# Second normalisation from turned rows, and loads dealt out in time, in a two-layer transformer kernel

## The chip, the cores and the metric

The kernel runs on one core of one Trainium2 chip, in one launch. The metric is the device time of the whole program in microseconds (us). The profile is of one execution; its engines are TensorE (PE, with its weight loads as PEld), VectorE (DVE), ScalarE (ACT), GpSimd (POOL) and the queue of SyncE (SPq), which here issues almost all DMAs.

## The reference, cut to what matters

Everything is float32. There are 4096 tokens of 128 features (16 sequences of 256).

```python
x  = L0_attn_x
xn = layernorm(x)                                   # no weights
x  = x + attn0(xn) + ffn0(xn)                       # layer 0
xn = layernorm(x)
x  = x + attn1(xn) + ffn1(xn)                       # layer 1

# attn0: normalises once more, with weights: h = (xn-mean)*rsqrt(var+eps)*ln_g + ln_b
#        8 heads of 64, rotary with scales, windows of 128 with both neighbours, softmax, w_out
# ffn0:  a shared MLP (128 -> 256 -> 128, gelu), and 8 experts of the same size, 2 of them for each token
# attn1: normalises once more, with ln_w and ln_b; u, v, base = silu(h @ uv_w.T + uv_b);
#        u * (relu(q.k/sqrt(128) + bias)^2 @ v) @ o_w.T
# ffn1:  32 experts of 64 with sigmoid gates in 4 groups, 8 for each token, and a shared MLP
```

What the change touches is the normalisation inside `attn0` and `attn1`: its input is already normalised, so its mean is zero and what is left is one factor for each token, `r2 = (var*rs*rs + eps)^-0.5`, where `rs` is the first normalisation's factor.

## The kernel before, in words

The tokens are handled in 8 groups of 512 (`g`). A group is a tile of 128 partitions by 4 chunks (`c`) of 128 features: token `c*128 + p` lies on partition `p`. Matmuls need it turned (features on partitions, 512 tokens along the row), which TensorE does with four 128x128 transposes (`transposed`, L179) into a PSUM bank; ScalarE copies it out.

**Layer 0, attention** (from the start to about 343 us). A loop over `s` from -3 to 64 handles one sequence and one pair of heads in each step; eight steps are a group. The order of the instructions on PE, DVE, ACT and POOL is the order in which they are written (`manual_schedule`); the order of SyncE's DMAs is left to a scheduler at build time. `routed(g)` makes the normalised rows `xn_all`, the factors `r2_all` and the turned rows `xnTs[g]`. `prepare(g)` then makes the input of the projections: `scaled` (L173) multiplies each of the four chunks by its tokens' factors on DVE, PE turns the result (L179), and ACT applies `ln_g` and `ln_b` while it copies the bank into `xhTs` (L358). So each group is turned twice, once as `xn` and once as `xh`. `rotated` makes queries and keys: PE multiplies (`pq`, L381), ACT copies to `here` (L391), four SyncE DMAs exchange halves of 32 partitions into `there` (L394), DVE combines (L398, L402). `load_rest` loads weights and the other groups' inputs, and from step 2 on 20 DMAs of a zero tile (L610) clear `x_rows`.

**Layer 0, experts** (about 346 to 443 us). GpSimd has scattered the tokens into `x_rows`, in 39 tiles of 256 rows, each of one expert. A loop over `t` has four stages, at the distances `at = [0, 4, 5, 6]`: `fetched` (SyncE reads the tile's expert number from a register and loads its weights `we` and its rows `xt`), `turned` (PE, L671; DVE copies to `xT`, L673), `hidden` (PE, L680; ACT gelu), and `down` (PE, L691; DVE adds a bias into `yt`, L698; SyncE stores `yt` to `y_rows`, L699). `we` and `xt` have 6 buffers each, `yt` 4. `rw2` (1 MB) and `rb2` (0.5 MB), which `down` needs, are loaded at `t == 2`. Eleven small weights of layer 1 (`wanted`) are loaded at every third `t`, and after the loop's text come `eg`, `eu` and `ed`, 1 MB each. Here every engine's order, SyncE's too, is the scheduler's.

**Layer 1** (about 443 us to the end). A prologue, in a written order, starts group 0; then a loop over the groups runs 17 pairs of expert matmuls (`g`, `u`, `z`: L960, L962, L997) with pieces of attention (`gau`) and of the next group's preparation (`finish0(g + 1)`) between them. `finish0` gathers the experts' rows, sums them into `x`, normalises (`xn`, L158), computes `r2` (`again`, L169), turns `xn` (L179) into `xnT`, computes `v` and the gates' scores (L791), then `scaled`, four more transposes and ACT's `ln_w1`, `ln_b1` make `xhT` (L817). `route1` chooses experts and spreads their weights over the partitions: a store to memory (L189) and loads that read a row of it for all partitions (`bc`, L865; four buffers, so that the last of a group's eight waits until pair 7 is done). In this loop only POOL's order is written by hand; PE, DVE, ACT and SyncE have the order that the scheduler chose.

Of the kernel before, what the change touches and what calls it, by code (L numbers as in the profile page):

```python
# [11 lines left out]
F32 = mybir.dt.float32  # L12
# [3 lines left out]
ALU = mybir.AluOpType  # L16
# [3 lines left out]
P = 128  # L20
B, N, D = 16, 256, 128
T = B * N
G = 512
# [24 lines left out]
def two_layers(ctx: ExitStack, tc: tile.TileContext, a: dict, out: bass.AP):  # L48
# [114 lines left out]
    def again(r2, var, rs, name):  # L163

        ve = small.tile([P, NC], F32, tag="bve2", name=f"bve2_{name}")
        nc.vector.tensor_tensor(ve, rs, rs, ALU.mult)
        nc.vector.tensor_tensor(ve, ve, var, ALU.mult)
        nc.vector.tensor_scalar(ve, ve, EPS, None, ALU.add)
        nc.gpsimd.tensor_tensor(r2, ve, mhalf, ALU.pow)  # L169

    def scaled(dst, src, r2):
        for c in range(NC):
            nc.vector.tensor_scalar(dst[:, c, :], src[:, c, :], r2[:, c : c + 1], None, ALU.mult)  # L173
# [158 lines left out]
    with first as pa:  # L332
# [17 lines left out]
        xhTs0, vs, oTs, heads, yps = {}, {}, {}, {}, {}  # L350

        def prepare(g):
            xh = wk.tile([P, NC, D], F32, tag="xh", name=f"xh_{g}")
            scaled(xh, xn_all[:, g * NC : (g + 1) * NC, :], r2_all[:, g, :])
            yield
            t = transposed(xh, f"xhT_{g}")
            xhT = wk.tile([P, G], F32, tag="xhT", name=f"xhTs_{g}")
            nc.scalar.activation(xhT, t, AF.Identity, bias=col("ln_b"), scale=col("ln_g"))  # L358
            xhTs0[g] = xhT
            vs[g] = wk.tile([P, NC, 512], F32, tag="v", name=f"v_{g}")  # L360
            yield
# [136 lines left out]
        NS = NG * 8  # L498
        sc, pTs, sms = {}, {}, {}
        order = mybir.EngineType  # L500
        with tc.manual_schedule(engines={order.PE, order.DVE, order.Activation, order.Pool}):
            routing = {g: routed(g) for g in range(NG)}
            preparing = {g: prepare(g) for g in range(NG)}

# [13 lines left out]
            for g in range(NG):  # L518
# [9 lines left out]
                    at = (b, b + 1, b + 2, b + 4, b + 6, b + 8, b + 9, *ranks)  # L528
                for n in at:
                    pieces.setdefault(n, []).append(g)  # L530
            turned_rows = {2: 7, 3: 12, 4: 22, 5: 27, 6: 37, 7: 47}

            step(routing, 0, 3)
            step(preparing, 0, 2)
# [12 lines left out]
            for s in range(-3, NS + 1):  # L547
# [14 lines left out]
                    sm = sms.pop(s + 1)  # L562
                    divided(s + 1, sc[s + 1][0], sm)

                if s == -2:
                    step(preparing, 1)
# [4 lines left out]
                for n in turned_rows:  # L571
                    if turned_rows[n] == s:
                        step(preparing, n)
                if s == 35:
                    placing = places0(wk)
# [62 lines left out]
    with ExitStack() as pb:  # L638
# [15 lines left out]

        def fetched(t):
            read(offs, t, tile_off, (E0 - 1) * P, mybir.EngineType.SP)
            we = wk.tile([P, W0], F32, tag="we", name=f"we_{t}", bufs=6)
            nc.sync.dma_start(out=we, in_=a["ex0"][bass.ds(offs[t], P), :])
            xt = wk.tile([P, 2, D], F32, tag="xt", name=f"xt_{t}", bufs=6)
            ins = nc.sync.dma_start(out=xt, in_=xr[t])  # L660
# [25 lines left out]
        def down(t, we, h):  # L686
            read(offs2, t, tile_w2, (E0 - 1) * 2 * D, mybir.EngineType.PE)
            yp = mm_tile(f"yr_{t}")[:, : 2 * D].rearrange("p (c d) -> p c d", d=D)
            for ch in range(2):
                for c in range(2):  # L690
                    nc.tensor.matmul(  # L691
                        yp[:, ch, :], h[:, c, ch * P : (ch + 1) * P], rw2[:, bass.ds(offs2[t] + c * D, D)],
                        start=(c == 0), stop=(c == 1),
                    )
            y = wk.tile([P, 2, D], F32, tag="yt", name=f"yt_{t}", bufs=4)
            read(offs3, t, tile_off, (E0 - 1) * P, mybir.EngineType.DVE)
            bias = rb2[:, bass.ds(offs3[t], D)].unsqueeze(1).to_broadcast([P, 2, D])
            nc.vector.tensor_tensor(y, yp, bias, ALU.add)  # L698
            nc.sync.dma_start(out=yr[t], in_=y)  # L699

        for g in range(2):
            for _ in shared0(g, wk):
                pass
        stage = [fetched, turned, hidden, down]
        at = [0, 4, 5, 6]
        state = {}

        wanted, w1 = [
# [9 lines left out]
            ("su", [P, P], None),  # L718
            ("sd", [P, D], None),
        ], {}  # L720
        for t in range(NT0 + at[-1]):
            if t == 2:
                rw2 = load("rw2", [P, E0, 2 * D], pool=wk, eng=nc.sync).rearrange("p e d -> p (e d)")
                rb2 = load("rb2", [P, E0 * D], src=a["rb2"].partition_broadcast(P), pool=wk, eng=nc.sync)
            if t % 3 == 0 and t // 3 < len(wanted):
                name, shape, src = wanted[t // 3]
                w1[name] = load(name, shape, src=src, pool=late, eng=nc.sync)
            for f, d in zip(stage, at):
                i = t - d
                if 0 <= i < NT0:  # L730
                    state[i] = f(i, *state.get(i, ()))
        uvu, uvv, uvb, vb, cosr, sinr, biasT, ow, sg, su, sd = (w1[name] for name, _, _ in wanted)
        eg = load("eg", [P, E1 // 2, P], pool=late, eng=nc.sync)
        eu = load("eu", [P, E1 // 2, P], pool=late, eng=nc.sync)
        ed = load("ed", [P, E1 // 2, D], pool=late, eng=nc.sync)


    with ExitStack() as pc:
# [14 lines left out]
        def finish0(g):  # L753
# [24 lines left out]
            again(r2, *normalise(xn, xs[g], *moments(xs[g], f"c{g}")), f"d{g}")  # L778
            nc.gpsimd.tensor_tensor(xs[g], xs[g], xn, ALU.add)
            yield  # L780
            t = transposed(xn, f"xn1T_{g}")
            xnT = wk.tile([P, G], F32, tag="xn1T", name=f"xn1Ts_{g}")
            nc.scalar.copy(xnT, t)
# [3 lines left out]
            if g:  # L787
                v = v1s[g] = wk.tile([P, NC, 256], F32, tag="v1", name=f"v1_{g}")
                for c in range(NC):
                    pv = mm_tile(f"pv1_{g}_{c}")  # L790
                    nc.tensor.matmul(  # L791
                        pv[:, : 256 + E1], xnT[:, c * P : (c + 1) * P], wvr, start=True, stop=True
                    )
                    nc.scalar.copy(sc[:, c, :], pv[:, 256 : 256 + E1])
                    nc.vector.scalar_tensor_tensor(
                        v[:, c, :], pv[:, :256], r2[:, c : c + 1], vbs, ALU.mult, ALU.add
                    )
                    if c % 2:
                        nc.scalar.activation(v[:, c - 1 : c + 1, :], v[:, c - 1 : c + 1, :], AF.Silu)
                    if c == 1:  # L800
                        yield
                sf = sc.rearrange("p c e -> p (c e)")
                nc.scalar.activation(sf, sf, AF.Sigmoid)
            else:
# [312 lines left out]
```

## Time and profile before

| | us |
|---|---|
| median of 6 runs | 940.52 (936.89 to 941.92) |
| the profiled execution | 941.32 |
| its span in the profile | 939.6 |
| PE busy | 893.0 (95%) |
| DVE busy | 695.5 (74%) |
| ACT busy | 495.8 (53%) |
| mean granted TensorE clock | 0.989 of full speed |

Between the span and the execution's own time lie 1.7 us, outside of all engines' work. A row of the timeline gives start, duration, engine, line, operation, output and inputs, and in brackets how long the engine was idle just before and what ended that. A row of the chain gives start, length, and the engine and line on the chain of work that ended last.

### The profile page before, as it was taken

The numbers are of one execution on the slowest core, as the hardware profiler recorded it, in microseconds if no ns is written. First come the engines' busy times: TensorE is split into PE (matmuls) and PEld (weight loads), VectorE is DVE, ScalarE is ACT, GpSimd is POOL, SyncE is SP. The second block draws the span as 40 slices with busy tenths as digits, with TensorE's granted clock in tenths as the row PEclk, the third lists the DMA queues.
The fourth block names the chain that finished last, engine by engine and source line by source line (L and its number), as shares of the span: only waits on it lengthen the run. The fifth ranks groups of instructions, "written<-read, shape, count | busy, mean of one in ns | idle before, by whom it ended". The sixth has DMA issues, their size and how long they took to land.

```text
span 939.6 us, 13471 instructions
## 1 busy us (share of the span) xinstructions
PE 893.0 (95%) x3762; PEld 508.4 (54%) x3762; DVE 695.5 (74%) x2283; ACT 495.8 (53%) x1228; POOL 280.3 (30%) x251
## 2 busy tenths in 40 slices
PE   2899999999999998988999999999999999999997
PEld 1556666555555547987445454454544545445453
DVE  4999999899999933332588587785877858778563
ACT  1788989798799863433443423444234441343411
POOL 2343433322467630000534222242222422221200
PEclk8899999999999999999999999999999999999999
DMA  6171010110122236875063433324333243331430
GB/s 198 26 236 40 23 35 23 24 35 23 44 79 70 64 97 209 249 220 170 29 136 85 104 93 78 91 68 103 96 77 91 65 104 96 75 91 45 104 90 11
DMA packets 69145, 84.54 MB, mean 90 GB/s; under 512 B 14800, under 2 KB 45264, under 8 KB 68560
## 3 DMA queue, kind: packets, MB, share of 16 engines
q1 hardware_dynamic: 64544, 74.76, 30.2%
q0 software_dynamic: 4096, 8.40, 2.8%
q8 instruction: 31, 0.51, 0.2%
q10 hardware_dynamic: 432, 0.53, 0.2%
q14 instruction: 42, 0.34, 0.1%
HBM read 58.22 MB, written 17.04 MB: 80 GB/s over the span
## 4 chain that ended last, share of the span: by engine, by line
PE 64%; DVE 18%; ACT 6%; DMA 4%; issue 3%; SPq 2%; POOL 1%; DVEq 0%; ACTq 0%
PE z L997 9%; PE u L962 8%; PE g L960 8%; PE s L421 5%; PE o L477 4%; DVE p L427 3%; PE yr L691 3%; PE h L680 3%; PE t L460 3%; PE o L935 3%; ACT r1s L901 2%; DVE p L446 2%; PE y L490 2%; PE pq L381 2%; PE pv L365 2%
## 5 line engine op out<-in xcount | busy, mean ns | idle before, releaser
L964 ACT ACTIVATE h<-g 128x512 f32<-128x512 f32 x128 | 75.1, 593 | 204.6 <-PE g L960 201.8
L966 DVE TENSOR_TENSOR h<-h,u 128x512 f32<-128x512 f32 x128 | 86.5, 681 | 61.8 <-PE u L962 46.3
L962 PE MATMUL u<-xn1Ts,eu 128*128 128x512 f32 x256 | 130.8, 592 | 1.2 <-DVE h L966 1.2
L960 PE MATMUL g<-xn1Ts,eg 128*128 128x512 f32 x256 | 130.8, 592 | 0.0
L437 ACT ACTIVATE p<-p,nm 128x256 f32<-128x256 f32 x256 | 127.5, 514 | 0.2 <-DVE nm L427 0.2
L997 PE MATMUL z<-h,ed 128*128 128x512 f32 x224 | 115.3, 598 | 1.7 <-DVE h L969 0.9
L758 POOL DMA_INDIRECT yg<-y_rows,slot_at x64 | 65.7, 1027 | 123.8 <-PE hs L627 105.2
L969 DVE TENSOR_TENSOR h<-h,bc 128x512 f32<-128x512 f32 x128 | 97.7, 770 | 2.3
L427 DVE CUSTOM_DVE_ANT_0 p<-s,mask 128x256 f32<-128x256 f32 x256 | 92.8, 417 | 2.6 <-PE s L421 2.6
L421 PE MATMUL s<-k,q 64*128 64x256 f32 x512 | 84.6, 412 | 9.2 <-DVE k L406 6.3
L962 PEld LDWEIGHTS u<-xn1Ts,eu 128*128 128x128 f32 x256 | 48.5, 190 | 61.2 <-issue 52.4
L460 PEld LDWEIGHTS t<-ident,p 128*128 128x128 f32 x512 | 59.4, 140 | 35.0 <-issue 8.6
L317 POOL DMA_INDIRECT x_rows<-xn_all,slot_at x64 | 67.1, 1048 | 37.0 <-ACT pT L467 16.0
L467 ACT COPY pT<-t 128x512 f32<-128x512 f32 x128 | 69.2, 597 | 10.4 <-PE t L460 10.4
L997 PEld LDWEIGHTS z<-h,ed 128*128 128x128 f32 x224 | 41.4, 190 | 56.0 <-issue 39.2
L960 PEld LDWEIGHTS g<-xn1Ts,eg 128*128 128x128 f32 x256 | 46.9, 190 | 45.3 <-issue 39.5
L906 POOL TENSOR_TENSOR r1s<-r1s,sinr 128x512 f32<-128x512 f32 x16 | 21.0, 1312 | 166.8 <-ACT r1s L901 143.3
L477 PE MATMUL o<-pT,v 128*64 128x256 f32 x512 | 70.1, 395 | 0.3 <-ACT oT L482 0.2
L460 PE MATMUL t<-ident,p 128*128 128x128 f32 x512 | 67.3, 274 | 1.4 <-ACT p L451 1.4
L421 PEld LDWEIGHTS s<-k,q 64*128 64x128 f32 x512 | 51.3, 189 | 27.2 <-DVE nm L427 9.2
L683 ACT ACTIVATE h0s<-h,we 128x256 f32<-128x256 f32 x78 | 32.7, 471 | 59.6 <-issue 36.7
L446 DVE TENSOR_SCALAR p<-p,sm 128x256 f32<-128x256 f32 x208 | 62.1, 357 | 2.3
(264 smaller groups left out, 1516.9 us busy)
## 6 DMA issues: line engine op xcount, KB each, us to landing
bc<-rows_r SPq DMA_DIRECT2D x128, 256.0 KB, 4.2
there<-here SPq DMA_DIRECT2D x128, 64.0 KB, 2.0
we<-in_ex_dram SPq DMA_DIRECT2D x39, 129.0 KB, 2.9
xt<-x_rows SPq DMA_DIRECT2D x39, 128.0 KB, 3.0
y_rows<-yt SPq DMA_DIRECT2D x39, 128.0 KB, 2.6
x_rows<-zero SPq DMA_DIRECT2D x19, 256.0 KB, 3.3
x<-in_x_dram SPq DMA_DIRECT2D x8, 256.0 KB, 5.8
out_dram<-out SPq DMA_DIRECT2D x8, 256.0 KB, 2.3
```

Source lines behind the costliest of these rows:

```text
L421: nc.tensor.matmul(sp[h][:, i, :], q[rows, b, i * P : (i + 1) * P], k[rows, b, :], start=True, stop=True)
L427: nc.vector.tensor_tensor_reduce(out=pr[:, h, i, :], in0=sp[h][:, i, :], in1=mask[:, i, :], scale=-1.0, scalar=-NEG, op0=ALU.add, op1=ALU. ...
L437: paces[1] = nc.scalar.activation(row, row, AF.Exp, bias=nm[:, n : n + 1], scale=-1.0, accum_out=sm[:, n : n + 1])
L446: nc.vector.tensor_scalar(row, row, sm[:, n : n + 1], None, ALU.mult)
L460: nc.tensor.transpose(tp[:, at : at + P], pr[:, h, i, j * P : (j + 1) * P], ident)
L477: nc.tensor.matmul(op[h * DH : (h + 1) * DH, :], vs[g][:, 2 * b + j, (2 * hp + h) * DH : (2 * hp + h + 1) * DH], pT[:, h, j, :], start=(j ...
L960: nc.tensor.matmul(gp, wg, xn1Ts[g], start=True, stop=True)
L962: nc.tensor.matmul(up, wu, xn1Ts[g], start=True, stop=True)
L964: nc.scalar.activation(h, gp, AF.Silu)
L966: nc.vector.tensor_tensor(h, h, up, ALU.mult)
L969: nc.vector.tensor_tensor(h, h, spread_w[g][n // 2][:, n % 2, :], ALU.mult)
L997: nc.tensor.matmul(zp, w, r, start=(n == 1), stop=False)
```

## The change

Four edits go together.

1. For all groups but the first, the second normalisation is applied to the turned rows that are there already. `row_stored` writes the 128x4 factors to memory (16 bytes from each partition), `row_spread` reads that row of 512 back into every partition, and `factored` multiplies the turned rows by it in one DVE instruction, whose second operand it reads with a step of 4 elements. The four `scaled` instructions and the four transposes of each of these groups are gone, in both layers; ACT's affine step now reads SBUF and writes in place.
2. In attention SyncE's order is written too: its DMAs go out in the order of the text.
3. In the expert loop `we` and `xt` have 10 buffers and `yt` 6, `turned`, `hidden` and `down` follow at 6, 7 and 8 tiles, and `rw2` and `rb2` are loaded at `t == 3`.
4. `eg`, `eu` and `ed` are loaded in quarters of 256 KB, at every even `t` from 6 to 28, and the small weights at odd `t` from 7 to 27.

```diff
+    def row_stored(r2, name):
+        d = rows.tile([P, NC], F32, tag="row", name=f"row_{name}")
+        nc.sync.dma_start(out=d, in_=r2)
+        return d
+
+    def row_spread(d, pool, name):
+        t = pool.tile([P, P, NC], F32, tag="xh", name=name)
+        nc.sync.dma_start(out=t, in_=d.rearrange("p c -> (p c)").partition_broadcast(P))
+        return t
+
+    def factored(dst, xT, t):
+        nc.vector.tensor_tensor(
+            dst.rearrange("f (c p) -> f c p", p=P), xT.rearrange("f (c p) -> f c p", p=P),
+            t.rearrange("f p c -> f c p"), ALU.mult,
+        )
...
         def prepare(g):
-            xh = wk.tile([P, NC, D], F32, tag="xh", name=f"xh_{g}")
-            scaled(xh, xn_all[:, g * NC : (g + 1) * NC, :], r2_all[:, g, :])
-            yield
-            t = transposed(xh, f"xhT_{g}")
-            xhT = wk.tile([P, G], F32, tag="xhT", name=f"xhTs_{g}")
+            if g:
+                d = row_stored(r2_all[:, g, :], f"a{g}")
+                yield
+                r = row_spread(d, wk, f"xh_{g}")
+                yield
+                xhT = t = wk.tile([P, G], F32, tag="xhT", name=f"xhTs_{g}")
+                factored(xhT, xnTs[g], r)
+            else:
...
             nc.scalar.activation(xhT, t, AF.Identity, bias=col("ln_b"), scale=col("ln_g"))
...
-        with tc.manual_schedule(engines={order.PE, order.DVE, order.Activation, order.Pool}):
+        with tc.manual_schedule(engines={order.PE, order.DVE, order.Activation, order.Pool, order.SP}):
...
-            turned_rows = {2: 7, 3: 12, 4: 22, 5: 27, 6: 37, 7: 47}
+            factors = {1: (-3, -2), 2: (4, 6), 3: (10, 12), 4: (18, 20), 5: (27, 29), 6: (34, 36), 7: (43, 45)}
...
-            we = wk.tile([P, W0], F32, tag="we", name=f"we_{t}", bufs=6)
+            we = wk.tile([P, W0], F32, tag="we", name=f"we_{t}", bufs=10)
...
-            xt = wk.tile([P, 2, D], F32, tag="xt", name=f"xt_{t}", bufs=6)
+            xt = wk.tile([P, 2, D], F32, tag="xt", name=f"xt_{t}", bufs=10)
...
-            y = wk.tile([P, 2, D], F32, tag="yt", name=f"yt_{t}", bufs=4)
+            y = wk.tile([P, 2, D], F32, tag="yt", name=f"yt_{t}", bufs=6)
...
-        at = [0, 4, 5, 6]
+        at = [0, 6, 7, 8]
...
+        weights1 = [(n, w, late.tile([P, E1 // 2, w], F32, tag=n, name=n)) for n, w in (("eg", P), ("eu", P), ("ed", D))]
+        quarters = [(q, *w) for w in weights1 for q in range(0, E1 // 2, 4)]
         for t in range(NT0 + at[-1]):
-            if t == 2:
+            if t == 3:
                 rw2 = load("rw2", ...
-            if t % 3 == 0 and t // 3 < len(wanted):
-                name, shape, src = wanted[t // 3]
+            if t >= 6 and t % 2 == 0 and quarters:
+                q, name, _, w = quarters.pop(0)
+                nc.sync.dma_start(out=w[:, q : q + 4, :], in_=a[name][:, q : q + 4, :])
+            if t >= 7 and t % 2 and (t - 7) // 2 < len(wanted):
+                name, shape, src = wanted[(t - 7) // 2]
...
-        eg = load("eg", [P, E1 // 2, P], pool=late, eng=nc.sync)
-        eu = load("eu", [P, E1 // 2, P], pool=late, eng=nc.sync)
-        ed = load("ed", [P, E1 // 2, D], pool=late, eng=nc.sync)
+        eg, eu, ed = (w for _, _, w in weights1)
...
             yield                                    # finish0, layer 1
+            if g:
+                row = row_stored(r2, f"b{g}")
             t = transposed(xn, f"xn1T_{g}")
...
+                r = row_spread(row, wk, f"xh1_{g}")
                 sf = sc.rearrange("p c e -> p (c e)")
                 nc.scalar.activation(sf, sf, AF.Sigmoid)
...
-            xh = wk.tile([P, NC, D], F32, tag="xh", name=f"xh1_{g}")
-            scaled(xh, xn, r2)
-            yield
-            t = transposed(xh, f"xh1T_{g}")
+            if not g:
+                xh = wk.tile([P, NC, D], F32, tag="xh", name=f"xh1_{g}")
+                scaled(xh, xn, r2)
+            yield
             xhT = wk.tile([P, G], F32, tag="xh1T", name=f"xh1Ts_{g}")
+            if g:
+                t = xhT
+                factored(xhT, xnT, r)
+            else:
+                t = transposed(xh, f"xh1T_{g}")
             nc.scalar.activation(xhT, t, AF.Identity, bias=col("ln_b1"), scale=col("ln_w1"))
```

In the built programs the order of the instructions on each engine can be read. In attention PE's order is that of before without the 28 transposes. In layer 1 it is that of before without the other 28, and at one place more: while PE waits for `xn` of the next group, the order before had put other matmuls before, between or behind the four `xn` transposes (in groups 0 to 6: three of 256 columns, one of 512, two of 512, one of 512, one of 512 and one of 256, none, three of 256); in the changed program there is none in any group.

More of the change, by code (lines that the diff above doesn't have):

```diff
@@ L352, in prepare @@
         def prepare(g):
-            xh = wk.tile([P, NC, D], F32, tag="xh", name=f"xh_{g}")
-            scaled(xh, xn_all[:, g * NC : (g + 1) * NC, :], r2_all[:, g, :])
-            yield
-            t = transposed(xh, f"xhT_{g}")
-            xhT = wk.tile([P, G], F32, tag="xhT", name=f"xhTs_{g}")
+            if g:
[6 more added lines that the diff above has]
+            else:
+                xh = wk.tile([P, NC, D], F32, tag="xh", name=f"xh_{g}")
+                scaled(xh, xn_all[:, g * NC : (g + 1) * NC, :], r2_all[:, g, :])
+                yield
+                t = transposed(xh, f"xhT_{g}")
+                xhT = wk.tile([P, G], F32, tag="xhT", name=f"xhTs_{g}")
             nc.scalar.activation(xhT, t, AF.Identity, bias=col("ln_b"), scale=col("ln_g"))
@@ L563, in two_layers @@
                     divided(s + 1, sc[s + 1][0], sm)
-                if s == -2:
-                    step(preparing, 1)
                 for n in pieces.get(s, ()):
@@ L570, in two_layers @@
                     step(preparing, g + 1)
-                for n in turned_rows:
-                    if turned_rows[n] == s:
+                for n in factors:
+                    if s in factors[n]:
                         step(preparing, n)
```

## The prediction

> **What bounds the kernel now.** I read the page first.
>
> ```profile
> span 939.6 us, 13471 instructions
> PE 893.0 (95%) x3762; PEld 508.4 (54%) x3762; DVE 695.5 (74%) x2283; ACT 495.8 (53%) x1228; POOL 280.3 (30%) x251
> ```
>
> TensorE is busy for 95%, so what can be won is either work taken from it or one of the few places where it stands. In windows of 10 us of attention, PE and DVE are both busy for 9.5 to 10 of 10: two engines at their limit. Then the chain of waits, in the expert loop of layer 0:
>
> ```profile
> 390.73 0.22 PE xtT L671 x2
> 390.95 0.86 PE h L680 x4
> 391.81 0.89 PE yr L691 x8
> 392.70 0.23 PE xtT L671 x2
> 392.94 0.30 SPq L660
> 393.28 0.45 SPq L76
> 393.82 8.25 DMA y_rows<-yt
> 402.37 0.16 issue
> 402.53 0.43 DVE xT L673
> 403.00 1.38 PE h L680 x4
> ```
>
> A tile costs PE 0.22 + 0.86 + 0.89 = 1.97 us, and 39 tiles 76.9; the loop takes from 351.2 (first transpose) to 442.7 (last `yr`), 91.5. The chain shows one reason: SyncE issues the 1 MB load of `eg` (L76) at 393.28, the store of `yt` behind it needs 8.25 us where its median is 2.6, and DVE, with four `yt` buffers, waits for it with the next tile's copy behind. The timeline of PE shows what that costs:
>
> ```profile
> 400.44 0.38 PE L671 MATMUL xtT<-ident,xt 128*128 128x128 f32 x2
> 403.00 1.38 PE L680 MATMUL h<-xT,we 128*128 128x256 f32 x4 [2.18 <-DVE xT L673]
> ...
> 428.80 0.38 PE L671 MATMUL xtT<-ident,xt 128*128 128x128 f32 x2
> 431.93 1.13 PE L680 MATMUL h<-xT,we 128*128 128x256 f32 x4 [2.74 <-DVE xT L673]
> ```
>
> Last, the places that the other edits touch: the start, layer 1 while it waits for `xn`, and the prices of what goes.
>
> ```profile
> 13.75 0.59 ACT L391 COPY here<-pq 128x512 f32<-128x512 f32 x1 [2.16 <-PE pq L381]
> 16.83 5.05 SPq L394 DMA_DIRECT2D there<-here  x8
> 21.00 0.69 DVE L402 TENSOR_TENSOR sq<-there,sinq 128x512 f32<-128x512 f32 x1 [1.37 <-DMA there<-here]
> ```
>
> ```profile
> 789.81 1.01 PE L179 MATMUL xn1T<-ident,xn 128*128 128x128 f32 x4 [0.89 <-DVE xn L158]
> 791.16 1.13 PE L997 MATMUL z<-h,ed 128*128 128x512 f32 x2 [0.34 <-DVE h L969]
> ```
>
> ```profile
> L173 DVE TENSOR_SCALAR xh<-xn_all,r_all x32: 270/278/286, 9.3 to 273.6; 128x128 f32<-128x128 f32 x32
> L179 PE MATMUL xh1T<-ident,xh x32: 272/273/273, 467.8 to 860.4; 128*128 128x128 f32 x32
> ```
>
> A transposing matmul is listed with 273 ns, but they overlap: in the chain four of them advance PE by 0.44 us. Four `scaled` take 0.79 us back to back.
>
> **Start (SyncE's order in attention).** Before, the copy `here` ends at 14.34, but the exchange goes out only at 16.83, behind loads that nothing needs yet; DVE waits 1.37 us for it. In the written order it goes first. Bounds 0 and 1.4 us. The loads it is moved past follow from 19.4 us on and took SyncE about 10 us (6.89 to 16.42, and two more later), so the third exchange, issued at 28.32 before, would come at 28 to 30.5 with the new row store (0.45 us) in front; its DVE reader stands at 35.5, and issue and landing take 4.4. I take 1.0.
>
> **Attention, factors.** For groups 1 to 7 PE loses 0.44 us each and DVE loses 0.79 and gains one 128x512 product; the nearest row, L402 with SBUF operands, takes 0.68 us and 0.60 back to back. The step of 16 bytes in its second operand is in no large row of this trace; bounds 0.60 (no effect) and 1.20 (half rate), and I take 0.60, since the broadcast forms of L202 and L204 (128x256 in 0.42) run at the plain rate. The Trainium skill, "SBUF — State Buffer", in the note on cachelines of its section "Door 1", speaks against this: reads that go to a new 16-byte line with every element pay a penalty. It gives no size; half rate would make DVE 0.4 us slower for each group instead of 0.2 faster. To about 229 us the chain runs over PE: five groups, 5 x 0.44 = 2.2 us; then over DVE: two groups at 0.19, 0.4. Together 2.6; bounds -2.8 (seven groups at half rate) and 5 (a bank of PSUM fewer in rotation, such as the 1.78 us that PE waited at 165.8). The row store and the spread hide: they are issued two steps (9 us) before their use, the nearest rows land in 1.8 us (`rows_r`, 16 KB) and 4.2 (`bc`, 256 KB), and `factored` follows two or more steps later. If SyncE stood instead, the exchanges behind it would be late, and DVE has no slack for that. The zero stores, now one for every two steps, are issued behind the exchange and not before it; they cost nothing before and after.
>
> **Expert loop.** Three stalls follow the 1 MB loads. From transpose to transpose: 400.44 to 408.49 for two tiles (8.05 - 3.94 = 4.1), 416.39 to 418.93 (0.6), 428.80 to 433.79 (3.0), together 7.7 us. A quarter holds a store up by a quarter of the excess (5.65 / 4 = 1.4 us), and six `yt` buffers are 11.8 us of cover. At the start PE stands from 354.2 to 357.2 and again until `rw2` is there; with `rw2` behind three tiles one more tile's transposes and `hidden` are done in that wait, 0.22 + 0.87 = 1.1. Sum 8.8. What hides this is DMA bandwidth: at `t` 6 to 28, 23 tiles of 385 KB with 3 MB of quarters and 1.3 MB of small weights, 13.5 MB in 45 us, 298 GB/s. The windows show 221 to 250 GB/s at a DMA share of 0.80 to 0.86 with tiles and small weights, and 325 to 340 at 0.93 with large loads, so about 1.0 of what there is. SyncE needs some 2.05 us for a tile with one more load (su at 389.14, sd at 391.23) against 1.97, and lags by 2 us more. Both are drawn from a lead of six tiles, 11.8 us less about 3 of landing. Bounds 4 and 10.7 us. The Trainium skill, "DMA: Bandwidth & Descriptors", section "Rules for kernel authors", asks for 1 MiB or more in one DMA; by it quarters would cost bandwidth. The rows say that here the large DMA itself is what the store waits behind.
>
> **Layer 1.** Four transposes less are 0.44 us a group. But PE's order loses what filled its wait for `xn`. The starts of the gated product (L943) are a group apart: 59.10, 58.15, 58.66, 58.25, 59.53, 58.25 us for groups 1 to 6. Group 5, which has no filler, is the slowest, and its wait is the one shown above; 59.53 - 0.44 = 59.09 for all six is 354.5 against 351.9, +2.6; group 0, like group 4, +0.8. Together 3.4 us slower; bounds -3.1 (fillers are worth nothing) and +10. The spread must be there when DVE comes to `factored`, at 800.2 in group 5. The last `bc` goes out at 792.5 to 793.0, `r2` is ready at 792.95, so store at 793.1, behind 512 KB of `bc` until about 797, spread at 797.1 and landed (3.6 to 4.2) at 800.7 to 801.3. DVE waited until 801.27 for the scores in any case, and 1.3 us more pass before PE misses the next `h`. I take nothing for it.
>
> **Sum.** 1.0 + 2.6 + 8.8 - 3.4 = 9.0 us; the profiled execution took 941.3 (span 939.6 and 1.7 around it), so 932.3. It stands 0.8 above the median, so 931.5.
>
> **Rivals.** *The loads saturate the queues.* If the loop moves only 227 GB/s, as around 380 us, 13.5 MB take 59.5 us, 14.2 more than the tiles, of which the lead covers 8.8: 5.4 lost, and 936.9. For it: the need is at the limit. Against: 325 to 340 GB/s were seen. *The factor comes late in layer 1 (slower).* If store and spread each take the longest landing of `bc`, 6.9 us, the spread is there at 793.1 + 6.9 + 0.6 + 6.9 = 807.5; DVE stands 7.3 us, 2.4 are covered, and seven groups lose 34: 966. It decides above 1.8 us of PE loss a group, (9.0 + 2.8) / 7 and the slack, a landing after about 804. For it: DVE's order is fixed, and the next pair's products are behind `factored`. Against: nothing else of SyncE's is in flight then. *It does not do what it says:* stalls of the expert loop were drift of engines that return elsewhere, and layer 1 costs more: 941, no change. *More comes:* layer 1 loses nothing and attention gives 5: 931.5 - 3.4 - 2.4 = 926.
>
> **How the numbers follow.** Forecast 0.60, saturation 0.12, more 0.10, no change 0.08, late factor 0.10. 0.3% (2.8 us) is about what a measurement can tell from no change. The forecast's own bounds, saturation (most of it below 937.7) and the rest give faster 0.82, same 0.08, slower 0.10. The range, 922 to 940, takes in all but the late factor and a tail of the best case.
>
> **What would show it.** In PE's timeline of the expert loop, no idle above 0.5 us after the third `xtT`, and 36 tiles at 1.97; groups of layer 1 at 59.1 in L943; a `factored` of about 0.68 us without a wait for its spread; DVE's first `sq` without its 1.37 us. Idle of DVE in front of `factored`, released by a DMA, or idle of PE released by `xt`, would prove it wrong.

## The result, and the profile after

The changed kernel takes 944.06 us (median of 24 runs, 939.56 to 948.07), the kernel before 940.23 beside it: a ratio of 1.0047 with a 95% interval of 1.0036 to 1.0059. It is 4 us slower, where 9 us faster was forecast. The profiled execution took 943.78 us, its span is 942.0.

The page of the changed kernel begins:

```profile
span 942.0 us, 13339 instructions
PE 884.7 (94%) x3706; PEld 500.2 (53%) x3706; DVE 694.7 (74%) x2241; ACT 495.7 (53%) x1228; POOL 283.1 (30%) x251
```

PE has 8.3 us less to do, as the change promised, and the span is 2.4 us longer. DVE has 42 instructions fewer and only 0.8 us less work. By stages, from the two traces:

| stage (ends with) | before, ends | after, ends | won | forecast |
|---|---|---|---|---|
| start (first `sq` of DVE begins) | 21.00 | 19.60 | +1.4 | +1.0 |
| rest of attention (last `y` of PE begins) | 342.86 | 346.03 | -4.6 | +2.6 |
| expert loop (last `yr` ends) | 442.67 | 441.12 | +4.7 | +8.8 |
| layer 1 (span ends) | 939.6 | 942.0 | -3.9 | -3.4 |

A window of each stage tells how long PE worked and how long it stood. In attention it worked 311.5 us before and 307.2 after, and stood 10.4 and 19.2; in layer 1 it worked 486.0 and 484.4, and stood 10.9 and 16.5. The two windows of the expert loop (length, then busy time and instructions of PE, PEld, DVE, ACT and POOL, granted clock, DMA share, GB/s):

```profile
342.86:442.67 99.81, 89.41 (x565) 79.05 (x564) 31.20 (x82) 37.52 (x85) 0.00 (x0) 0.97 0.70 213
346.03:441.12 95.09, 86.61 (x565) 76.49 (x564) 31.76 (x82) 37.45 (x85) 0.00 (x0) 1.00 0.75 224
```

PE has the same 565 instructions in both. So only 1.9 of the 4.7 us won here are standing (10.4 and 8.5); 2.8 are PE's own work, at a granted clock of 0.97 before and 1.00 after.

**Attention.** The summary of the line of `factored`, the longer half of it (duration as minimum, median, maximum in ns, first and last start):

```profile
L185 DVE TENSOR_TENSOR xhTs<-xnTs,xh x7: 1061/1090/1115, 39.9 to 282.3; 128x512 f32<-128x512 f32 x7
...
  DMA xh<-row_b: 3.2, 6
...
  ACT xhTs L386: 11.7, 7
```

It takes 1.09 us and not 0.68; DVE waits for the spread 6 times in layer 1, 3.2 us in all; ACT waits for the product 11.7 us in 7 times. What PE waited for behind `divided_last` in attention, before (L451) and after (L479), in us in total, times, and the longest:

```profile
PE t L460 <- ACT p L451: 1.4, 2, 0.9
PE t L488 <- ACT p L479: 9.0, 7, 3.3
```

These are 7.6 of the 8.8 us that PE stood longer. The timelines of DVE, ACT and PE around one of the seven show what stands behind that (in brackets the idle time before, and its releaser):

```profile
81.09 1.09 DVE L185 TENSOR_TENSOR xhTs<-xnTs,xh 128x512 f32<-128x512 f32 x1
82.21 0.81 ACT L386 ACTIVATE xhTs<-xhTs,vec 128x512 f32<-128x512 f32 x1 [1.68 <-DVE xhTs L185]
82.93 0.49 ACT L479 ACTIVATE p<-p,sm 128x256 f32<-128x256 f32 x1
83.48 0.55 PE L488 MATMUL t<-ident,p 128*128 128x128 f32 x3 [1.32 <-ACT p L479]
```

`divided_last` (L479) has its input, but on ACT it stands behind the affine step (L386), which stands for 1.68 us behind `factored`; PE then stands 1.32 us in front of the transposes of `p`. Before, ACT's affine step read a bank that PE had filled at the start of the step, and the profile lists no idle time of ACT in front of it but the first time.

**Expert loop.** The chain of waits, and PE's timeline at two of the six places where it stood after the fourth tile (0.33, 1.71, 0.46, 0.45, 1.75 and 0.38 us):

```profile
377.67 4.40 DMA eu<-in_eu_dram
382.07 0.02 issue
382.08 0.34 SPq L757
```

```profile
388.82 0.41 PE L698 MATMUL xtT<-ident,xt 128*128 128x128 f32 x2 [1.71 <-DMA xt<-x_rows]
...
407.96 0.41 PE L698 MATMUL xtT<-ident,xt 128*128 128x128 f32 x2 [1.75 <-DMA xt<-x_rows]
```

The idle that the prediction named as proof against it is there: PE released by `xt`, 5.1 us. The chain says why: SyncE issues a quarter of `eu` at 377.67, it lands 4.40 us later, and only then does the next quarter go out. Between the two lie seven other DMAs of SyncE (`we`, `xt`, the store of `yt`, a small weight, and `we`, `xt`, the store of `yt` again). In the built program every DMA of SyncE waits until an earlier one has landed, in a rotation of eight: the next quarter is the eighth DMA after the quarter. So two tiles can't take less than the landing of a quarter (medians of 4.4 to 4.6 us, one of 5.98 at 401.13), where PE needs 3.94. SyncE's issues alone aren't it: they fill 4.0 of the 4.41 us from 377.67 to 382.08, and between 366 and 411.5 us its queue stood 5.6 us for landings.

**Layer 1.** PE's waits for `xn` in all of layer 1, before and after; then its timeline where it comes to the transposes of `xn`, in group 3, and DVE's ten us later:

```profile
PE xn1T L179 <- DVE xn L158: 2.3, 4, 0.9
PE xn1T L198 <- DVE xn L158: 6.6, 7, 1.3
```

```profile
732.60 1.01 PE L198 MATMUL xn1T<-ident,xn 128*128 128x128 f32 x4 [0.88 <-DVE xn L158]
733.95 1.12 PE L1036 MATMUL z<-h,ed 128*128 128x512 f32 x2 [0.34 <-DVE h L1008]
```

```profile
743.50 1.09 DVE L185 TENSOR_TENSOR xh1Ts<-xn1Ts,xh 128x512 f32<-128x512 f32 x1 [0.58 <-DMA xh<-row_b]
```

The groups are 59.15, 59.08, 59.26, 59.09, 59.08 and 59.09 us apart, each with this wait; 59.09 was forecast. PE's waits in front of `z`, the second line of the timeline, grew from 0.9 us in 3 times to 2.6 in 8.

### The profile page after: what moved, and what is told of

Read it like the earlier page. It is cut to its first block, busy times and chain, and to the rows that moved or that the text cites. A ratio compares the mean times of both kernels' runs of the same rounds, so it can differ in the third digit from the quotient of the medians.

```text
span 942.0 us, 13339 instructions
## 1 busy us (share of the span) xinstructions
PE 884.7 (94%) x3706; PEld 500.2 (53%) x3706; DVE 694.7 (74%) x2241; ACT 495.7 (53%) x1228; POOL 283.1 (30%) x251
## 4 chain that ended last, share of the span: by engine, by line
PE 50%; DVE 28%; ACT 9%; DMA 5%; issue 4%; POOL 1%; SPq 1%; DVEq 0%; ACTq 0%; POOLq 0%
PE z L1036 8%; PE u L1001 7%; PE g L999 7%; DVE p L455 5%; DVE p L474 4%; PE o L974 3%; DMA xt<-x_rows 3%; ACT r1s L940 2%; PE s L449 2%; PE yr L718 2%; PE o L505 2%; PE h L707 2%; DVE h L1008 2%; ACT p L465 2%; PE z L1054 2%
## 5 line engine op out<-in xcount | busy, mean ns | idle before, releaser
L449 PE MATMUL s<-k,q 64*128 64x256 f32 x512 | 81.6, 412 | 8.0 <-DVE k L434 4.5
L488 PEld LDWEIGHTS t<-ident,p 128*128 128x128 f32 x512 | 59.4, 141 | 44.8 <-ACT p L479 12.2
```

The source lines that it names most:

```text
L449: nc.tensor.matmul(sp[h][:, i, :], q[rows, b, i * P : (i + 1) * P], k[rows, b, :], start=True, stop=True)
L488: nc.tensor.transpose(tp[:, at : at + P], pr[:, h, i, j * P : (j + 1) * P], ident)
```

## The experiments

Several of these executions ran at a lower granted clock than the two above (a mean of 0.977 to 0.992), with dips between 270 and 320 us whatever the kernel; so ratios are taken against runs of the kernel before on the same chip, and stages are compared where the clock was full. For attention that is rotations 8 to 16, from about 84 to 165 us; a "rotation" is one start of `sq` on DVE, and four make a group. The length of the expert loop scatters with the clock too. The loop of before takes 96.3 to 100.9 us in its six profiles, and in five of them PE runs at a granted clock of 0.5 for 3.4 to 10.2 us of it; so the idle of PE says more there than the length.

### The parts by themselves

`attention_only`, `loop_only` and `layer1_only` are the kernel before with the hunks of edits 1 and 2 in attention, of edits 3 and 4, and of edit 1 in layer 1.

> Edits 1 (attention's half) and 2 alone on the kernel before. Theory A (the loss of attention is its own): the last `y` of attention ends about 3.2 us later than before, as in the changed kernel (346.10 against 342.93), and the kernel is 2.5 to 4 us slower. Rival (the loss is a random drift between two executions, or comes from the other edits): within 1.5 us of before. The prediction on record put this part at 3.6 us faster.

> Edits 3 and 4 alone on the kernel before. Theory: the loop's gain is 4.7 us, as from 8.2 us (342.93 to 351.17 and on) the trace of the changed kernel shows between attention's end and the last `yr` (99.7 us before, 95.0 after); the kernel is 4 to 5.5 us faster, and idle of PE released by `xt` stays at 5 to 7 us. Rival (the prediction's own sum): 8.8 us faster, if the stalls came only because attention had ended later.

> Edit 1 in layer 1 alone on the kernel before. Theory: groups of 59.1 us in place of 58.2 on the average, 3.4 to 4 us slower, with PE idle in front of the transposes of `xn` in each group. Rival: the scheduler gives this kernel another order on PE than the whole change has, the filler stays, and it is within 1 us of before.

Measured: 1.0074 (1.0043 to 1.0105), 0.9941 (0.9919 to 0.9963) and 1.0008 (0.9980 to 1.0037). So attention's loss is its own. Its profile fell at a clock of 0.977, so the end of its attention says nothing; against `affine_later` below it runs parallel from rotation 9 on. The loop alone takes 93.4 us (447.44 - 354.09), with PE waiting 3.5 us for `xt`, 2.4 of them after the fourth tile: less than the 5 to 7 us that the first theory expected, and not none. Layer 1 missed: its groups are 58.55 us apart on the average of six, against 58.60 before. The built orders tell why: in this kernel PE does the attention product `o` around and between the transposes of `xn`, in the changed kernel nothing. The same source gives two orders, as the scheduler's choice depends on what comes ahead.

### Attention: the wait, or DVE's time

`affine_later` is `attention_only` with the affine step one step of the loop after the product:

```diff
                 factored(xhT, xnTs[g], r)
+                yield
...
-                if r == 0:
+                if r == 0 or r == 1 and g >= 0:
                     step(preparing, g + 1)
```

> As attention_only, but ACT's affine step is written one step of the loop after `factored`, so that `divided_last` no longer stands behind an instruction that waits for DVE. Theory H (ACT's order is the cost: PE's transposes of `p` wait for `divided_last`, which waits behind the affine step, which waits 1.68 us for `factored`): the 11.4 us of idle on PE in attention fall to about 6, and 3 to 4 us of the loss go; the kernel is within 1 us of before. Rival D (DVE's price is the cost: 1.09 us for `factored`, where four `scaled` took 0.79, and the ACT wait only shows DVE's lateness): less than 1 us is won against attention_only, as DVE is the bound.

The ratio is 1.0026 (0.9994 to 1.0057), half a per cent better than `attention_only`, with intervals that overlap; but in rotations 8 to 16 it wins only 0.37 us of the 0.93 that the changed kernel loses there. The new place has a wait of its own: the next product `pq` follows in the same step, and PE now waits for the affine step. Neither theory was told apart. Two more kernels take the price of the product: `contiguous` stores the factors as four rows of 128, so that `factored` reads them without a step, and `factor_on_pool` does so too and puts the product on GpSimd.

```diff
-        d = rows.tile([P, NC], F32, tag="row", name=f"row_{name}")
-        nc.sync.dma_start(out=d, in_=r2)
+        d = rows.tile([NC, P], F32, tag="row", name=f"row_{name}")
+        nc.sync.dma_start(out=d.rearrange("c p -> p c"), in_=r2)
...
-        nc.vector.tensor_tensor(... t.rearrange("f p c -> f c p"), ALU.mult)
+        nc.gpsimd.tensor_tensor(dst, xT, t.rearrange("f c p -> f (c p)"), ALU.mult)   # nc.vector in contiguous
```

> affine_later, with `factored` on DVE, but the factors stored as four rows of 128, so that the second operand is read without its step of 16 bytes. Theory S (the step sets the duration): `factored` takes 0.68 us and not 1.09, and a group of attention is 0.1 to 0.2 us shorter than before where it was 0.2 longer. Rival (two large SBUF operands beside GpSimd's work set it): 1.0 us or more, no change. The store now writes 512 pieces of 4 bytes; it may land later than 1.8 us, which nothing waits for.

> affine_later, with `factored` of attention on GpSimd and the 512 factors stored as four rows of 128, so that the operand is read without a step. Theory D (DVE is the bound of attention, and each us on DVE is a us of time): DVE loses four `scaled` (0.79 us) and gains nothing, so between the rotations 9 and 25 (94.8 to 255.7 us before) each of the four groups is 0.8 us shorter than before, 3 us in all, where affine_later was 0.8 us longer in all. Rival P (PE is the bound, as the prediction had it): 0.44 us a group, 1.8 in all. Rival W (GpSimd is late, and DVE or ACT waits for its small powers): longer than before.

`contiguous`, its product and its SyncE at the start:

```profile
L185 DVE TENSOR_TENSOR xhTs<-xnTs,xh x7: 678/683/686, 44.0 to 286.8; 128x512 f32<-128x512 f32 x7
```

```profile
29.74 0.38 SPq L174 DMA_DIRECT2D row_a<-r_all  x1
30.23 2.42 SPq L420 DMA_DIRECT2D there<-here  x4
37.02 0.33 SPq L180 DMA_DIRECT2D xh<-row_a  x1
```

Without the step the product takes 0.683 us: theory S holds for the duration. Its groups are not shorter than before (+0.15 us in rotations 8 to 16). The store now consists of 512 pieces of 4 bytes (the page counts 2688 more packets under 512 B than that of `affine_later`, 7 x 384), the spread behind it could go out only 7.3 us later, and SyncE stood for it with the next exchange behind: both kernels lose some 4 us before rotation 3, and "nothing waits for it" was wrong. The ratios are 1.0093 (1.0060 to 1.0126) and 1.0147 (1.0073 to 1.0220). On GpSimd the product misses theories D and P (+0.66 us in rotations 8 to 16, where D said -1.6). Rival W has the sign, but not the reason: in these rotations neither DVE nor ACT waits for GpSimd. The timelines of DVE and GpSimd say what does:

```profile
124.51 1.97 DVE L472 TENSOR_SCALAR p<-p,sm 128x256 f32<-128x256 f32 x3
124.53 1.28 POOL L185 TENSOR_TENSOR xhTs<-xnTs,xh 128x512 f32<-128x512 f32 x1
```

The three scalings of DVE take 0.88 us elsewhere; while GpSimd multiplies they take 1.97. At six of the seven products a scaling meets GpSimd's product and ends 0.15 to 0.16 us after it; at the seventh (248.7 us) DVE reads `pq` and isn't slowed. So DVE pays for most of the product in any case. The Trainium skill, "SBUF — State Buffer", section "Who interferes with whom", has a rule for this: the two engines share a pair of ports, `tensor_scalar` is among the DVE instructions that can take the pair, and whichever engine comes second is blocked until the first has done. The ends of the scalings here agree with it.

Last, the place. In `early_stepped` the product is written one step ahead (the last step of the group before), the affine step stays where it was, group 1 is made as before, and SyncE's loads in the expert loop are moved (next section). `early_contiguous` is the same without the step of 16 bytes, and `order_and_pool_loads` has SyncE's order but no factors at all.

```diff
-            if g:
+            if g > 1:
...
                 factored(xhT, xnTs[g], r)
+                yield
...
-            factors = {1: (-3, -2), 2: (4, 6), 3: (10, 12), 4: (18, 20), ...}
+            factors = {1: (-2,), 2: (4, 6, 7), 3: (10, 12, 15), 4: (18, 20, 23), ...}
```

> loop_pool, and edit 2 (SyncE's order in attention) alone, with no factors. Theory: the first exchange goes out 2.5 us earlier and DVE's first `sq` is 1.1 to 1.4 us earlier than in loop_pool; the third exchange waits behind the loads, so 1.0 to 1.4 us remain at the end of attention and no more. Rival: the written order delays later exchanges and attention ends where it did (340.9 in loop_pool). The loop stays at 90 us, layer 1 at 58.4 us a group.

> order_and_pool_loads with the factors of attention for groups 2 to 7 (group 1 as before), `factored` as in the change (16-byte step) but in the last step of the group before, so that ACT's affine step one step later finds it done and nobody waits for it. Theory D (DVE's time is what counts): DVE has 1.09 - 0.79 = 0.3 us more a group, six groups 1.8 us later at attention's end than order_and_pool_loads. Theory H (only the waits cost): not later; 0.44 us a group earlier if PE is the bound, 2.6 in all.

> early_stepped with the factors stored as four rows of 128, so that `factored` takes 0.68 us (0.60 back to back). Theory D: DVE has 0.60 - 0.79 = -0.2 us a group, attention ends 1.1 us earlier than in order_and_pool_loads and 2.9 earlier than in early_stepped. Theory H: the same end as early_stepped. No wait of SyncE for the store (4.3 us once in contiguous), since it is spread two steps later and group 1 needs none.

How late DVE's rotations start, in us against `loop_pool`, whose attention is that of before and whose clock was 0.999 (from DVE's timelines):

| kernel | rotation 1 | 8 | 16 | 8 to 16 |
|---|---|---|---|---|
| changed kernel | -1.14 | +1.38 | +2.31 | +0.93 |
| `affine_later` | -1.12 | +1.37 | +1.93 | +0.56 |
| `factor_on_pool` | -1.28 | +7.30 | +7.96 | +0.66 |
| `contiguous` | -1.30 | +6.57 | +6.72 | +0.15 |
| `order_and_pool_loads` | -1.11 | -1.06 | -1.05 | +0.01 |
| `early_stepped` | -1.12 | -0.81 | -0.80 | +0.01 |
| `early_contiguous` | -1.04 | -0.62 | -1.42 | -0.80 |

Rotations 8 to 16 are two groups. The place of the product costs 0.93 - 0.01 = 0.92, 0.46 us a group, and over rotations 8 to 24, four groups at full clock, it is the same: +2.29 against +0.40 in `early_stepped` and +0.32 in `early_again` (below). PE's waits say it too: in rotations 8 to 16 it doesn't stand at all in `loop_pool`; in the changed kernel it stands 1.7 us, in two waits in front of the transposes of `p`.

In the same two groups the step of the operand costs 0.01 + 0.80 = 0.81, 0.40 a group, which is the difference of the durations (1.09 - 0.68), and with both mended the product wins 0.40 us a group against four `scaled` and four transposes, the size that the prediction had put in. That is shown for these two groups only. From rotation 16 to 24 `early_contiguous` loses 3.4 us, where `order_and_pool_loads`, with a dip of the clock at the same place, loses 1.6; and `contiguous`, at full clock, loses 2.7, where `affine_later` loses 1.4. Why the shorter product doesn't pay there is not settled; its store of 512 pieces is one candidate.

By rotation 8 the changed kernel is 2.2 us behind `early_stepped` (+1.38 against -0.81). Little of it is group 1, which has factors in one and not in the other: at rotation 7 they are 0.15 apart (-0.41 and -0.56), and the rest comes behind the changed kernel's second product at 81.09.

Of the whole kernels `order_and_pool_loads` is at 0.9877 (0.9851 to 0.9902), `early_stepped` at 0.9933 (0.9908 to 0.9958), `early_contiguous` at 0.9969 (0.9939 to 0.9999). These put `early_stepped` behind `order_and_pool_loads`, with intervals that don't meet, but all three profiles also lost time late in attention. The first two were run again side by side:

> order_and_pool_loads once more, beside early_again on one chip, as the granted clock moved both profiles late in attention. Expected: 0.987 to 0.990 of before.

> early_stepped once more, beside order_again. Theory D (DVE's 0.3 us a group counts in full): 1.8 us slower than order_again. Theory H (only waits cost, and PE's 0.44 us a group come through in part): 0 to 2.6 us faster than order_again.

0.9899 (0.9841 to 0.9957) and 0.9907 (0.9872 to 0.9942): this time no difference that can be measured. Theory D's 1.8 us would be 0.2%, which these intervals don't exclude; rotations 8 to 16 do (-0.01 us in `early_again`, where D says 0.6), and 8 to 24 (+0.32, where D says 1.2). The 0.44 us a group that theory H hoped for didn't come through either.

### The expert loop: SyncE's line, or the bytes

`loop_pool` is `loop_only` with the quarters and small weights issued by GpSimd:

```diff
+        def paced(t, ins):
+            if t >= 7:
+                tc.add_manual_dep(ins.ins, copies[t - 7].ins.name, ...)     # the copy xT of tile t - 7
...
-                nc.sync.dma_start(out=w[:, q : q + 4, :], in_=a[name][:, q : q + 4, :])
+                paced(t, nc.gpsimd.dma_start(out=w[:, q : q + 4, :], in_=a[name][:, q : q + 4, :]))
```

> loop_only, with the 12 quarters and the 11 small weights issued by GpSimd, each after the copy `xT` of the tile seven behind, so that the same bytes move at about the same times and SyncE issues only `we`, `xt` and `yt`. Theory L (SyncE's line is the bound: a DMA is issued only when the eighth one before it has landed, and a quarter that takes 4.4 to 4.6 us to land is the eighth one before the next quarter, so two tiles take 4.5 us and more where PE needs 3.94): no idle of PE released by `xt` after the third tile, and the loop (last `y` of attention to last `yr`) takes 91 us, where loop_only takes 93.3 and the changed kernel 95.0. Rival B (the prediction's rival: 13.5 MB saturate the DMA engines): `xt` lands as late as before, idle for `xt` stays at 2.5 to 6 us, the loop at 93 to 95.

Windows of `loop_pool`:

```profile
370.00:380.00 10.00, 10.00 (x74) 9.48 (x73) 3.78 (x10) 4.19 (x10) 2.80 (x6) 1.00 0.97 305
380.00:390.00 10.00, 10.00 (x74) 9.48 (x73) 3.78 (x10) 4.30 (x11) 2.85 (x6) 1.00 0.95 308
```

The loop takes 90.1 us, and after the fourth tile PE never stands, at 305 to 308 GB/s and a DMA share of 0.95 to 0.97. In the changed kernel PE stood at 229 to 264 GB/s and 0.76 to 0.89. `xt` even lands later than in the changed kernel (median 4.6 us against 3.4); it is issued early enough. Theory L holds, and the bytes are not the bound. That a quarter waits for the one before because both write the same tile is excluded too: GpSimd issues its quarters 3.95 us apart (366.11, 370.06, 374.01), while each takes some 5 us to land. The kernel is at 0.9911 (0.9876 to 0.9945), not told apart from `loop_only` by the ratio alone. In the profiles of six other kernels with loads on GpSimd the loop takes 88.1 to 89.6 us, in two (`whole_pool_loads`, `mended_stepped`) 91.2 and 92.5. In none of these nine does PE wait for `xt` after the fifth tile; in the three with SyncE's loads it does, for 5.1 us (the changed kernel), 2.4 (`loop_only`) and 2.4 (`sums_earlier`, below, whose loop is the changed kernel's and takes 90.7).

> The changed kernel with one thing moved: the quarters and small weights issued by GpSimd, paced by the tiles. Layer 1 has the order without filler again (59.1 us a group) and attention's factors stand as in the change. Expected: the loop (last `y` of attention to last `yr`) falls from 95.1 to 90 us, so 5 us less than the changed kernel, and 2 to 3 us less than before (0.997 of it). If SyncE's line were not the cause, 943 to 944 as now.

In the changed kernel itself the same edit shortens the loop from 95.1 to 91.2 us, one profile of each; the waits for `xt` after the fourth tile are gone. The ratio is 1.0009 (0.9981 to 1.0038), 0.4 of a per cent below the changed kernel's own but not the 0.997 expected: attention and layer 1 lose as before, and this profile lost another 6.7 us between rotations 27 and 32, where the granted clock dipped.

### Layer 1: PE's order, or the factors

`sums_earlier` is the changed kernel with the sums of the next group one pair earlier.

```diff
-                        for _ in range({4: 1, 5: 2, 7: 2, 8: 1, 9: 2}.get(n, 0)):
+                        for _ in range({3: 1, 4: 2, 7: 2, 8: 1, 9: 2}.get(n, 0)):
```

> The changed kernel, with the transposes of `yT` and the sums of the next group written one pair of layer 1 earlier (3 and 4 instead of 4 and 5), so that `xn` is ready before PE comes to its transposes. Theory O (what layer 1 loses is the wait for `xn` in PE's order without filler, 0.88 and 0.34 us a group): groups of 57.9 us in place of 59.1, 8 us less in the whole. Rival C (DVE is as full there, and the sums push the products of the expert pairs back, so that PE waits for `h` instead): 59 us as now.

1.0110 (1.0069 to 1.0151): rival C holds. The groups are 59.3 to 59.4 us apart, and 61.3 in the three in which the granted clock fell to 0.5 for 3.4 us. The wait for `xn` is gone; in its place DVE comes to `factored` earlier and stands 2.42 us for the spread, and PE 1.8 us for `h`. `all_mended` is `early_contiguous` with the factors in layer 1, and `mended_stepped` the same with 16-byte pieces; both have PE's `o` around the transposes of `xn`, as `layer1_only`.

> early_contiguous with the factors in layer 1 too, stored as rows. Its built order has other matmuls of PE around the transposes of `xn` (the attention product `o` in groups 1 to 6), which the changed kernel lacks. Theory O (the loss of layer 1 was that order, not the factors): groups of 58.2 to 58.6 us, layer 1 as before or up to 1 us shorter, and the kernel within 1 us of early_contiguous, 12 us faster than before. Rival: the factors cost layer 1 their DVE time and the wait for the spread, 59.1 us a group.

> all_mended with the factors stored as in the change, 16 bytes from each partition. Theory T (in all_mended the store of 512 pieces of 4 bytes was late: 10.2 us from its issue to that of the spread behind it, then 8.2 us of idle on DVE in front of `factored`, 7 us a group): the store lands in about 3 us, and with the order of PE that has `o` between the transposes of `xn` a group takes 58.2 to 58.7 us, as before; the whole is within 1.5 us of early_again. Rival (the factors themselves cost layer 1, and the changed kernel's 59.1 would stand): 59.1 or more.

`all_mended` is at 1.0465 (1.0409 to 1.0521). Its timelines of SyncE, DVE and PE in one group:

```profile
762.16 0.55 SPq L174 DMA_DIRECT2D row_b<-brs  x1
772.39 0.34 SPq L180 DMA_DIRECT2D xh<-row_b  x1
```

```profile
776.11 0.69 DVE L185 TENSOR_TENSOR xh1Ts<-xn1Ts,xh 128x512 f32<-128x512 f32 x1 [8.24 <-DMA xh<-row_b]
...
780.50 2.07 PE L1042 MATMUL z<-h,ed 128*128 128x512 f32 x2 [6.49 <-DVE h L1014]
```

The store of 4-byte pieces takes 10.2 us until the spread can go out, DVE stands 8.24 us in front of `factored`, the products of the expert pairs behind it are late, and PE stands 6.49 us; then it works at a granted clock of 0.50 from 778.9 to 785.5. Groups are 65.6 us on the average of six, against 58.60. This is the prediction's slower rival, which the change itself escaped. With 16-byte pieces (`mended_stepped`, 0.9931, 0.9898 to 0.9965) the group is back at 59.28 us, which is the rival's side of what was expected: theory T explains 6.3 of the 7.0 us, and DVE still stands 2.3 us for the spread (13.6 us in 6 groups), after which PE waits 1.06 us for `z`. Where PE's order has filler, DVE comes to the product sooner and the spread is late; where it has none, PE waits for `xn` first and the spread is nearly in time. `layer1_only`, with a like order and 1.8 us of such idle on DVE, loses nothing, while `mended_stepped` loses 0.7 us a group: in front of `z` PE waits 1.9 us in 4 times in the one, 7.4 us in 7 times in the other. Why the half us of a later spread brings that wait is not settled.

## Why the prediction was wrong

- **Start: right.** 1.0 was taken, 1.4 measured at the first `sq`; in `order_and_pool_loads` 1.1 of it is still there at rotation 16, in its repetition `order_again` only 0.1.
- **Attention: wrong, 7.2 us** (+2.6 forecast, -4.6 measured, outside its lower bound of -2.8). Two steps failed. "I take 0.60" for a product with a step of 16 bytes: it takes 1.09, nearly the half rate of the upper bound. The note on cachelines that spoke against the change (the Trainium skill, "SBUF — State Buffer", section "Door 1") was right, with 1.09 us against 0.683 without the step, and the broadcast forms that the prediction went by have another pattern. And "`factored` follows two or more steps later" asked only when its input is there, not who stands behind its reader: the affine step waits on ACT for the product, with `divided_last` and so PE's transposes behind it (9.0 us of waits, 1.4 before). The 0.44 us of PE a group were real in the two groups where they could be read (0.40 in `early_contiguous`), but in the changed kernel the place (0.46) and the step (0.40) took twice that. Seven groups at the 0.46 us of rotations 8 to 16, or the 0.57 of 8 to 24, are 3.3 to 4.0 of the 4.6 us; the rest isn't assigned.
- **Expert loop: half right** (8.8 forecast, 4.7 measured, of which 1.9 are standing). The three stalls went, as forecast. But they were 2.18, 0.30 and 2.74 us of standing, 5.2 and not 7.7: most of the rest of the 4.1 us from 400.44 to 408.49 is PE at work at a granted clock of 0.5 (403.7 to 407.2), right behind its stall, which the prediction counted with the stall. After, no such stretch fell into the loop, and that gave the other 2.8 us. Whether it would, the prediction didn't ask; such stretches follow some stalls and not others, so this share of the gain is in part luck. In `loop_pool` PE stands 4.9 us in the loop (10.4 before). What was mis-sized is SyncE's time: "some 2.05 us for a tile" counts issues, and leaves out that an issue waits for the eighth DMA before it. The saturation rival named the right symptom (PE released by `xt`, 5.4 us priced and 5.1 measured) with the wrong cause.
- **Layer 1: right in size** (-3.4 forecast, -3.9 measured; groups of 59.09 forecast and measured), with PE's wait for `xn` in each group, as forecast. DVE did wait for the spread, 0.53 us in each of six groups, which the prediction had named as a sign against it; the groups are as long as it put them without that. That PE's order alone makes the loss is argued and not shown: `mended_stepped`, with other matmuls around the transposes, loses as much by another wait.
- One figure of the late factor's threshold is off: (9.0 + 2.8) / 7 is 1.7 us a group, not 1.8. It decides nothing.

The sum of what was measured, 1.4 - 4.6 + 4.7 - 3.9 = -2.4, is the difference of the two spans. What beats both kernels is SyncE's order with edits 3 and 4 and GpSimd's loads, without the factors: 0.9877 and, again, 0.9899 of the kernel before. `loop_pool`, without SyncE's order, is at 0.9911, which these intervals don't tell apart.

## What to carry to other kernels

Cost an instruction that is moved by who stands behind its reader in each engine's order, not by whether its input is there; here the same product cost 0.46 us a group or nothing, one step of the loop apart. A queue that may have only so many DMAs outstanding (eight here) is slowed by the landing time of its largest one, so background loads belong on another queue than the transfers that the loop waits for. Where a scheduler chooses the order, read the built order of the kernel that is run: the same edit gave two orders in layer 1, with and without a loss.

## What was not expected of the hardware

- A DVE product of 128x512 float32 whose second operand has a step of 16 bytes takes 1.09 us, without the step 0.683.
- Twelve times in the expert loops of the 18 profiles the granted clock of TensorE fell to 0.5, for 3.4 us (6.8 in two), each time within 2.2 us of the end of a stall of PE of 1.6 us or more; about as many such stalls have no such stretch.
- Three DVE scalings of 128x256 take 1.97 us in place of 0.88 while GpSimd multiplies 128x512 in SBUF.
- A store of 2 KB as 512 pieces of 4 bytes holds the read behind it back by 7.3 and 10.2 us; as 128 pieces of 16 bytes it lands in 1.6 to 4.1 us in the changed kernel's trace. The Trainium skill, "DMA: Bandwidth & Descriptors", section "Rules for kernel authors", says that a last dimension that isn't contiguous becomes one descriptor for each element, and agrees.
